# Substitution of 32-wide blocks: GpSimd in place of VectorE

## The chip, the cores and the metric

The kernel runs on one core of a Trainium2 chip. The metric is the device time of one execution in microseconds (us). A core has five engines that run their own queues of instructions, each in the order in which the program holds them: TensorE (PE in the profile; its weight loads are listed apart as PEld), VectorE (DVE), ScalarE (ACT), GpSimd (POOL) and SyncE (SP), which here only issues DMA transfers. Semaphores order the engines among each other.

## The reference

One transformer block on x of shape (8, 256, 256): 8 sequences of 256 tokens of 256 channels. A layernorm with shift and scale from a condition vector, a gated linear-attention layer, a gated residual, a second such layernorm, a feed-forward layer with 2:4 sparsified hidden values, and a second gated residual. What matters here is the recurrence of the attention layer, for 16 key heads, each with two value heads of width 128:

```python
def step(S, inp):
    q_t, k_t, v_t, b_t, d_t = inp
    Sk = jnp.einsum('bhi,bhipj->bhpj', k_t, S)
    dv = b_t[..., None] * (v_t - Sk)
    upd = jnp.einsum('bhi,bhpj->bhipj', k_t, dv)
    S = S * d_t[:, :, None, :, None] + upd
    o = jnp.einsum('bhi,bhipj->bhpj', q_t, S)
    return (S, o)
```

with q and k from a projection, a causal convolution of four taps and an l2 norm, v from projection and convolution, b a sigmoid, and d a decay between 0 and 1. The output o is rms-normed, multiplied by a gate silu(z) and projected back.

## The kernel before

The kernel does not step through the tokens. It cuts each sequence into chunks of 128 tokens and solves each chunk as a triangular system: with a strictly triangular matrix A of products of keys, decays and b, it needs the inverse of (I + A). That inverse is built in two parts. First, the 32 x 32 blocks on the diagonal of all matrices of a group are inverted by substitution; then two levels of small matmuls join blocks of 32 to blocks of 64 and blocks of 64 to 128.

The work is ordered in groups. A group is four key heads (GH = 4) of a pair of sequences; there are 4 pairs and 16 heads, so 16 groups. A head of a pair has 2 sequences x 2 chunks x 2 value heads = 8 matrices, a group 32, and each matrix has four diagonal blocks of 32: 128 blocks, one for each partition. The steps, by the names in the code:

- stage_a, for each head: the key projection (ps_k, L432), the convolution (convolved: one ScalarE instruction at L418 and three VectorE instructions at L420), the norms, the table diag (GpSimd, L516) and the power nk (GpSimd, L523), the scan e (VectorE, L551), and the matrices a_t (L563). The diagonal blocks of a_t are written to a scratch area scr in device memory (L572).
- stage_b, once for each group: one load (L585) brings the 128 blocks, each as a 32 x 32 square in its own partition, into the tile blk; GpSimd sets the diagonal (L587); then 30 steps of substitution follow, step j with two VectorE instructions: tmp, the outer product of j values of column j and 31 - j values of row j (L604), and its subtraction from the block of j rows and 31 - j columns (L610). Each instruction needs the result of the one before it. After step 16 and after the last, the helper turn lets ScalarE write a transposed negative copy xb (L592) and a negated blk (L597); after the last, SyncE issues the stores of both to scr_x (L596) and scr_y (L599).
- levels, for two heads at a time: loads of the inverted blocks from scr_x and scr_y (x_even at L690 and others), then matmuls ps_w (L707, L710), ps_t, ps_w2 and ps_t2, with the finished inverses in t_inv.
- prepare, for each head: projections of query and values (ps_qv, L432) with their convolutions cv (L418, L420), the gate (ps_z, L646; gz, L653), and a scale eps_q (GpSimd, L657).
- attend, for each head and sequence: matmuls with the inverse (L804, L847) and others, sums of squares ss (VectorE, L858), the reciprocal root rs (GpSimd, in the helper at L105), and the product of output, rs and gate og (VectorE, L871).
- shares and turned: the output projection (ps_y, L901), added to y (L912).
- feed_forward, for the tokens of sequences whose attention is complete: its work is spread over later groups; in it the VectorE instructions of the sparsification (L211 to L229). It uses the same GpSimd helper at L105 for rstd. The last pair's feed-forward runs alone at the end.

While the heads of one group are in attend, stage_a and stage_b of the next group are mixed in as background: the function along, called once for each round of the heads' generators, advances the background by a work count, in which a yield of stage_a counts 3.0 and a step of the substitution 1.0, so that it is due by the middle of the group. The levels for the first two heads of a group run within the last head of the group before, the levels for the other two in its second head. The order in which the instructions of an engine finally stand is fixed when the program is built, by a scheduler that goes by the order of the code and by its own timing of each instruction (L1210). The first group has nothing to be mixed with: its stage_a runs step by step in first_group, its substitution follows at once, and the heads' first projections are tied behind it with issue_after.

Of the kernel before, what the change touches and what calls it, by code (L numbers as in the profile page):

```python
# [48 lines left out]
def adaln_block(  # L49
# [18 lines left out]
    nc = tc.nc  # L68
# [297 lines left out]
    with ExitStack() as scope:  # L366
# [210 lines left out]
        def stage_b(scr, scr_x, scr_y):  # L577

            blk = single.tile([P, Q, Q], F32, tag="blk", name="blk")
            nc.sync.dma_start(out=blk, in_=scr)  # L585
            xb = single.tile([P, Q, Q], F32, tag="xb", name="xb")
            nc.gpsimd.memset(blk.rearrange("p a b -> p (a b)")[:, :: Q + 1], -1.0)  # L587
            yield

            def turn(rows):  # L590

                nc.scalar.activation(  # L592
                    xb[:, rows], blk[:, :, rows].rearrange("p b a -> p a b"), AF.Copy, scale=-1.0
                )
                if rows.stop == Q:
                    nc.sync.dma_start(out=scr_x, in_=xb)  # L596
                nc.scalar.activation(blk[:, :, rows], blk[:, :, rows], AF.Copy, scale=-1.0)  # L597
                if rows.stop == Q:
                    nc.sync.dma_start(out=scr_y, in_=blk)  # L599

            for j in range(1, Q - 1):
                m = Q - 1 - j
                tmp = single.tile([P, j, m], F32, tag="tmp", name="tmp", bufs=2)
                nc.vector.tensor_tensor(  # L604
                    out=tmp,
                    in0=blk[:, j, None, j + 1 :].to_broadcast([P, j, m]),
                    in1=blk[:, 0:j, j, None].to_broadcast([P, j, m]),
                    op=ALU.mult,
                )
                solved = nc.vector.tensor_tensor(  # L610
                    out=blk[:, 0:j, j + 1 :], in0=blk[:, 0:j, j + 1 :], in1=tmp, op=ALU.subtract
                )
                yield solved.ins
                if j == Q // 2:
                    turn(slice(0, Q // 2))
            turn(slice(Q // 2, Q))
            yield
# [321 lines left out]
        def first_group(filled, recs, scratch):  # L939
# [34 lines left out]
            for done in stage_b(scr, *scratch):  # L974
                last[0] = done or last[0]

        def ahead(g, recs, scratch):

            bp, k0 = groups[g]
            scr = scratch_of(scratch)  # L980
            h_bp = tokens(bp)
            wk = single.tile([P, GH, CC, P], F32, tag="wk", name="wk")
            nc.sync.dma_start(out=wk, in_=w_keys[k0 // GH])

            waiting = []
            for hp in range(GH + 1):
                if hp < GH:
                    waiting.append(stage_a(k0 + hp, bp, hp, wk, h_bp, scr))
                    recs.append(next(waiting[-1]))
                    yield 3.0  # L990
                if hp > 0:
                    for _ in waiting.pop(0):
                        yield 3.0
            for done in stage_b(scr, *scratch):
                last[0] = done or last[0]
                yield 1.0
# [217 lines left out]
```

## Time and profile before

| | |
|---|---|
| median of 3 runs | 2111.28 us (2106.41 to 2114.01) |
| the profiled execution's own time | 2106.59 us |
| its span, first to last instruction | 2104.6 us |
| mean granted TensorE clock | 0.991 of full speed |
| TensorE busy | 2000.5 us (95%) |
| VectorE busy | 1666.0 us (79%), 4039 instructions |
| ScalarE busy | 1271.3 us (60%) |
| GpSimd busy | 391.1 us (19%), 376 instructions |

A busy time is the time in which at least one instruction of that engine was on record; matmuls are pipelined, and their ends are modelled. A row of a group names line, engine, operation, output and inputs by the program's names, shapes and count, then the busy time in us and the mean duration of one in ns, and behind the second bar the idle time of the engine just before these instructions and what ended it. A row of stretches gives for each engine the busy time and, in brackets, the number of instructions. A row of a timeline gives the start in us, the duration in us, and in square brackets the idle time before and what ended it; a row may cover several instructions in succession.

### The profile page before, as it was taken

How to read it: one execution, taken by the hardware profiler on the slowest of the kernel's cores; microseconds unless marked ns; L12 is line 12 of the kernel's file. 1: busy time of each engine (PE TensorE's matmuls, PEld its weight loads, DVE VectorE, ACT ScalarE, POOL GpSimd, SP SyncE). 2: the span in 40 equal slices, each digit the busy share in tenths (PEclk: the TensorE clock that was granted, in tenths of full speed). 3: DMA queues.
4: the chain of work that ended last, by engine and by line, in shares of the span. 5: the costliest groups of instructions: out<-in, count | busy, mean ns of one | idle time of the engine just before them, and what ended most of it. 6: DMA issues, size and time to landing. Idle time of an engine off the chain costs nothing. (4 is left out here: it accounts for less than half of the span.)

```text
span 2104.6 us, 45727 instructions
## 1 busy us (share of the span) xinstructions
PE 2000.5 (95%) x16684; PEld 1583.3 (75%) x16684; DVE 1666.0 (79%) x4039; ACT 1271.3 (60%) x4260; POOL 391.1 (19%) x376
## 2 busy tenths in 40 slices
PE   8999999899999999999999989999999999999998
PEld 5567777677778777777777777777777877777877
DVE  6778887878788787788878779787978869787557
ACT  3557677766656556566665655657566655656652
POOL 3121312112121211212021121211213121121110
PEclk9999999999999999999999999999999999999999
DMA  4342414333343544434444443443444343344226
GB/s 127 99 131 72 117 55 108 99 80 105 92 115 103 125 115 102 123 105 111 140 92 111 107 123 113 114 115 99 128 110 115 97 127 110 94 121 116 66 91 218
DMA packets 356257, 230.99 MB, mean 110 GB/s; under 512 B 286265, under 2 KB 297913, under 8 KB 356033
## 3 DMA queue, kind: packets, MB, share of 16 engines
q1 hardware_dynamic: 336160, 167.53, 30.7%
q10 hardware_dynamic: 19872, 60.54, 9.3%
q8 instruction: 132, 2.16, 0.4%
q14 instruction: 93, 0.75, 0.1%
HBM read 188.38 MB, written 29.12 MB: 103 GB/s over the span
## 5 line engine op out<-in xcount | busy, mean ns | idle before, releaser
L420 DVE SCALAR_TENSOR_TENSOR cv<-ps_qv,conv_sb,cv 128x510 f32<-128x510 f32 (+2 forms) x564 | 409.4, 739 | 88.1 <-ACT cv L418 84.4
L432 PE MATMUL ps_qv<-h_bp,wh 128*128 128x512 f32 x768 | 365.7, 602 | 8.4 <-DVE cv L420 7.1
L105 POOL TENSOR_TENSOR rs<-ss,minus_halves 128x4 f32<-128x4 f32 x128 | 147.9, 1163 | 942.3 <-DVE ss L858 941.8
L646 PE MATMUL ps_z<-wh,h_bp 128*128 128x256 f32 x1024 | 252.1, 387 | 17.7 <-DVE cv L420 17.2
L901 PE MATMUL ps_y<-wo,og_p 128*128 128x256 f32 x1024 | 236.3, 380 | 2.6 <-ACT gz L653 2.2
L646 PEld LDWEIGHTS ps_z<-wh,h_bp 128*128 128x128 f32 x1024 | 186.9, 193 | 49.1 <-DVE cv L420 22.4
L838 ACT ACTIVATE junk<-o 128x128 f32<-128x128 f32 x512 | 154.2, 305 | 112.1 <-DVE o L854 96.8
L432 PEld LDWEIGHTS ps_qv<-h_bp,wh 128*128 128x128 f32 x768 | 134.3, 193 | 112.7 <-issue 100.2
L901 PEld LDWEIGHTS ps_y<-wo,og_p 128*128 128x128 f32 x1024 | 188.2, 190 | 27.7 <-ACT gz L653 3.3
L604 DVE TENSOR_TENSOR tmp<-blk 128x30 f32<-128x30 f32 (+14 forms) x480 | 156.9, 327 | 56.4 <-DMA blk<-scr 48.7
L418 ACT ACTIVATE cv<-ps_qv,conv_sb 128x512 f32<-128x512 f32 x188 | 129.3, 689 | 107.5 <-PE ps_qv L432 106.8
L516 POOL TENSOR_TENSOR diag<-consts,bk 128x1032 f32<-128x1032 f32 x64 | 123.5, 1929 | 364.5 <-DVE bk L507 329.1
L420 DVE SCALAR_TENSOR_TENSOR k_t<-ps_k,conv_sb,k_t 128x510 f32<-128x510 f32 (+1 forms) x189 | 139.8, 741 | 37.6 <-ACT k_t L418 35.6
L610 DVE TENSOR_TENSOR blk<-blk,tmp 128x30 f32<-128x30 f32 (+14 forms) x480 | 156.8, 327 | 9.6
L551 DVE TENSOR_TENSOR_SCAN e<-dbc,diag 128x1032 f32<-128x1032 f32 x60 | 138.1, 2302 | 19.5 <-POOL diag L516 13.4
L871 DVE SCALAR_TENSOR_TENSOR og<-o,rs,gz 128x128 f32<-128x128 f32 x512 | 145.8, 344 | 8.4 <-POOL rs L105 7.7
L812 PE MATMUL ps_ks<-u,cross 128*128 128x128 f32 x1024 | 141.7, 280 | 7.1 <-ACT u L806 3.9
L812 PEld LDWEIGHTS ps_ks<-u,cross 128*128 128x128 f32 x1024 | 128.7, 193 | 16.6 <-issue 6.3
L190 PE MATMUL ps_ff<-h,w_ff 128*128 128x128 f32 x1024 | 132.5, 277 | 4.2 <-ACT h L149 2.3
L190 PEld LDWEIGHTS ps_ff<-h,w_ff 128*128 128x128 f32 x1024 | 124.4, 192 | 14.9 <-issue 5.9
L778 ACT ACTIVATE vn<-ps_v,nk 128x256 f32<-128x256 f32 x256 | 104.5, 486 | 51.4 <-PE ps_v L773 51.2
L826 ACT ACTIVATE o<-ps_ks,g_in 128x128 f32<-128x128 f32 x256 | 79.9, 365 | 87.2 <-DVE rr L817 78.5
(180 smaller groups left out, 4189.9 us busy)
## 6 DMA issues: line engine op xcount, KB each, us to landing
wh<-in_w_heads ACTq DMA_DIRECT2D x64, 640.0 KB, 4.5
w_ff<-in_w_ff SPq DMA_DIRECT2D x128, 256.0 KB, 3.1
dbc<-d_dram SPq DMA_DIRECT2D x60, 516.0 KB, 3.7
wo<-in_w_heads ACTq DMA_DIRECT2D x32, 512.0 KB, 3.7
w_dn<-in_w_down SPq DMA_DIRECT2D x64, 256.0 KB, 3.0
wk<-in_w_keys SPq DMA_DIRECT2D x16, 512.0 KB, 3.5
scr<-a_t SPq DMA_DIRECT2D x256, 32.0 KB, 2.1
blk<-scr SPq DMA_DIRECT2D x16, 512.0 KB, 4.5
```

Of the source, the lines that this page charges most:

```text
L105: nc.gpsimd.tensor_tensor(out=out, in0=in_, in1=minus_halves[:, :n], op=ALU.pow)
L190: nc.tensor.matmul(ps[:, a, l, :], lhsT=w[:, k, l, :], rhs=h2[:, k, :], start=(k == 0), stop=(k == CC - 1),)
L420: nc.vector.scalar_tensor_tensor(out=dst[:, :, d:], in0=ps[:, :, : T - d], scalar=taps[:, KC - 1 - d : KC - d], in1=dst[:, :, d:], op0=ALU ...
L432: nc.tensor.matmul(ps.rearrange("p b t -> p (b t)"), lhsT=w[k], rhs=h_bp[:, k, :], start=(k == 0), stop=(k == CC - 1),)
L551: nc.vector.tensor_tensor_scan(e.rearrange("p i s t -> p (i s t)"), dbc.rearrange("p i f -> p (i f)"), diag.rearrange("p s t -> p (s t)"), ...
L604: nc.vector.tensor_tensor(out=tmp, in0=blk[:, j, None, j + 1 :].to_broadcast([P, j, m]), in1=blk[:, 0:j, j, None].to_broadcast([P, j, m]), ...
L610: solved = nc.vector.tensor_tensor(out=blk[:, 0:j, j + 1 :], in0=blk[:, 0:j, j + 1 :], in1=tmp, op=ALU.subtract)
L646: nc.tensor.matmul(ps[:, n, :], lhsT=h_bp[:, k, i * T + n * P : i * T + (n + 1) * P], rhs=wh[:, k * 640 + 384 : (k + 1) * 640], start=(k = ...
L812: nc.tensor.matmul(ps_ks[:, ct, h, :], lhsT=cross[:, h, ct, :], rhs=u0[:, h, :], start=True, stop=True)
L838: nc.scalar.activation(junk, o[:, n, h, :], AF.Square, accum_out=ss[:, n, h : h + 1])
L871: nc.vector.scalar_tensor_tensor(out=og[:, n, h, :], in0=o[:, n, h, :], scalar=rs[:, 2 * n + h : 2 * n + h + 1], in1=gz[:, i, n, h, :], op ...
L901: nc.tensor.matmul(ps_y[:, n, :], lhsT=og_p[:, j // 2, i, n, j % 2, :], rhs=wo[:, j // 2, j % 2, :], start=(j == 0), stop=(j == 3),)
```

## The change

The two instructions of a substitution step are issued to GpSimd (nc.gpsimd) where they were issued to VectorE (nc.vector). Operands, shapes and the order of the code stay as they are.

```diff
             for j in range(1, Q - 1):
                 m = Q - 1 - j
                 tmp = single.tile([P, j, m], F32, tag="tmp", name="tmp", bufs=2)
-                nc.vector.tensor_tensor(
+                nc.gpsimd.tensor_tensor(
                     out=tmp,
                     in0=blk[:, j, None, j + 1 :].to_broadcast([P, j, m]),
                     in1=blk[:, 0:j, j, None].to_broadcast([P, j, m]),
                     op=ALU.mult,
                 )
-                solved = nc.vector.tensor_tensor(
+                solved = nc.gpsimd.tensor_tensor(
                     out=blk[:, 0:j, j + 1 :], in0=blk[:, 0:j, j + 1 :], in1=tmp, op=ALU.subtract
                 )
                 yield solved.ins
```

## The prediction

> **What bounds the kernel now.** I read the page's busy times and groups first, then the busy times of single stretches, the waits, and the timeline at both ends of the substitution.
>
> ```profile
> PE 2000.5 (95%) x16684; PEld 1583.3 (75%) x16684; DVE 1666.0 (79%) x4039; ACT 1271.3 (60%) x4260; POOL 391.1 (19%) x376
> ...
> L604 DVE TENSOR_TENSOR tmp<-blk 128x30 f32<-128x30 f32 (+14 forms) x480 | 156.9, 327 | 56.4 <-DMA blk<-scr 48.7
> ...
> L516 POOL TENSOR_TENSOR diag<-consts,bk 128x1032 f32<-128x1032 f32 x64 | 123.5, 1929 | 364.5 <-DVE bk L507 329.1
> ...
> L610 DVE TENSOR_TENSOR blk<-blk,tmp 128x30 f32<-128x30 f32 (+14 forms) x480 | 156.8, 327 | 9.6
> ```
>
> TensorE carries the span, and no other engine is near it on average. POOL looks empty, and DVE would lose 156.9 + 156.8 = 313.7 us. But an average says nothing of the stretch in which the substitution runs. Its 960 instructions come in 16 bursts of 60 (one per group). The first burst stands alone in the startup; the 15 others I cut out by the first and last L604/L610 of each and asked for the busy times of those stretches, first all instructions (two stretches and the sum shown), then those on blk alone (the sum):
>
> ```profile
> core 0: us, PE busy (x) PEld busy (x) DVE busy (x) ACT busy (x) POOL busy (x), PEclk, DMA share, GB/s
> 147.10:191.60 44.50, 40.51 (x259) 32.53 (x259) 40.77 (x124) 31.69 (x104) 4.99 (x7) 1.00 0.12 32
> 1385.90:1427.30 41.40, 40.36 (x259) 32.74 (x259) 38.60 (x121) 24.65 (x86) 6.24 (x8) 1.00 0.38 110
> sum 640.80, PE 608.99 PEld 496.30 DVE 597.48 ACT 396.54 POOL 85.51; mean PE 40.60 PEld 33.09 DVE 39.83 ACT 26.44 POOL 5.70
> ...
> sum 640.80, DVE 293.39 ACT 26.25 POOL 2.28; mean DVE 19.56 ACT 1.75 POOL 0.15
> ```
>
> A stretch lasts 640.8/15 = 42.7 us on average. In it DVE is busy 39.8 us (93%), 19.6 of them with the substitution; POOL has 5.7. So in a third of the span DVE is as full as TensorE, and it is there that the change acts. TensorE is idle 640.8 - 609.0 = 31.8 us in all the stretches together: the most that a freer DVE can give back there.
>
> What hangs on the end of a burst is the next thing to see. At 1427 us (ScalarE's and SyncE's timelines):
>
> ```profile
> 1427.34 1.10 ACT L592 ACTIVATE xb<-blk 128x512 f32<-128x512 f32 x1 [1.36 <-DVE blk L610]
> ...
> 1428.47 0.32 SPq L596 DMA_DIRECT2D scr_x<-xb  x1
> 1429.61 0.32 SPq L599 DMA_DIRECT2D scr_y<-blk  x1
> 1431.11 1.83 SPq L690 DMA_DIRECT2D x_even<-scr_x  x4
> ```
>
> ScalarE sits waiting for the last L610, copies, the copy goes out, and the load of x_even follows as soon as it can; the levels' matmuls (L707, L710), which open the next group's work, wait for that load 14.2 us in total by the answer for L690 (6.1, 3.2, 2.8 and 2.1). The burst's end is thus on the path, with next to no slack: a burst that ends later moves the levels, and before them ScalarE (other copies are queued behind L592) and SyncE's queue (the loads behind L596).
>
> **What a substitution step costs on POOL.** The trace has two POOL multiplies of the same make (one input repeated along rows, the other along elements): diag, 1032 elements, median 1918 ns, and taps, 512 elements, 1041 ns (L1012). The line through them is 177 ns + 1.687 ns per element. One burst is two instructions of j(31 - j) elements for j = 1 to 30, that is 2 x 4960 = 9920 elements: 60 x 0.177 + 9920 x 0.001687 = 10.6 + 16.7 = 27.4 us, against 19.6 on DVE. Every step needs the one before; the trace shows no POOL instruction that waits for its predecessor on POOL. Bounds: 0 (nk follows diag without a gap) and 0.1 us (rs starts 0.09 us after the ss that DVE wrote); DVE's own chain has 0.03. I take 0.05: 3.0 us, so 30.4 us per burst, 0.51 per step. The upper bound for the fixed part is eps_q (L657), a POOL instruction of 4 elements with mean 387 ns (24.8 us for 64): 60 x 0.21 = 12.6 us more. The rows of a step are short (30 rows of one element at j = 30) and diag's are 129 long; no row prices that, and this upper end has to cover it.
>
> The Trainium skill, "GPSIMD Engine Reference", section 3, holds VectorE to be about 1.96 times faster for two-input elementwise work; by that ratio a burst would be an estimated 19.6 x 1.96 = 38 us instead of 30, and the final time some 120 us higher than mine. The diag row is of this very kernel, so I keep it.
>
> **What the move makes late.** On POOL a step shares the queue with rs, eps_q and rstd, and it shares something with DVE:
>
> ```profile
> 370.29 1.92 POOL L516 TENSOR_TENSOR diag<-consts,bk 128x1032 f32<-128x1032 f32 x1 [1.45 <-DVE bk L507]
> ...
> 370.66 1.58 DVE L500 TENSOR_SCALAR n2k<-n2k 128x4 f32<-128x4 f32 x1
> ...
> 1971.06 3.27 POOL L105 TENSOR_TENSOR rs<-ss,minus_halves 128x4 f32<-128x4 f32 x2 [20.41 <-DVE ss L858]
> ...
> 1971.70 0.42 DVE L223 TENSOR_TENSOR mag<-mag,c 128x256 f32<-128x256 f32 x1
> 1972.03 0.42 DVE L224 SCALAR_TENSOR_TENSOR mag<-mag,c 128x256 f32<-128x256 f32 x1
> ```
>
> The DVE instruction of 4 elements takes 1.58 us (others of its kind 0.16) and ends with diag; in the other direction two rs take 3.27 us (about 1.03 each elsewhere) while DVE works through a run of instructions whose inputs all lie in SBUF. DVE instructions with an input in PSUM (cv L420, 742 ns beside POOL and 740 without) show nothing of it. So POOL and DVE's all-SBUF instructions exclude each other. The same page, section 8, says that the two share their SBUF interfaces, with contention for DVE instructions of two SBUF inputs; that speaks against this change, which puts 60 such POOL instructions in each stretch that until now had about seven.
>
> How much: in the stretch 1385.9 to 1427.3, DVE's all-SBUF instructions besides the substitution are og 4.6 us, the sparsification and feed-forward tail (L168 to L253) 5.5, ss 0.6: 10.7 us. In the four stretches before the first feed-forward there are only og and ss, 5.2. Mean (11 x 10.7 + 4 x 5.2)/15 = 9.2 us in which POOL stands still.
>
> **The sum for a stretch.** POOL: 30.4 + 5.7 (its own work) + 9.2 (locked out) = 45.3 us against the 42.7 that the stretch lasts: 2.6 us longer, times 15 = 39 us. DVE falls from 39.8 to 20.3 us plus its waits for a POOL step in progress (some 12 runs of all-SBUF instructions at up to 0.45 us, 5 us): it has room, and the rs that are late by a step or more are caught by that room, except where og (L871) waits at the head of DVE's queue with cv behind it; POOL's length counts that already. Of TensorE's 31.8 us idle in the stretches I give back 10: the waits view puts only some of it on DVE (cv 17.2 + 7.1 in the whole span), the rest on ScalarE and loads.
>
> **The startup.** The first burst runs from 60.6 to 83.8 us, almost by itself (19.9 of 23.2 us), and its levels start at 89.9. On POOL it takes 30.4 + 1.6 (two rstd and an eps_q between) = 32 us: 9 us later. TensorE has key projections of the next group to bring forward (it does them at 86.3), but they are bounded by ScalarE's and DVE's part; I count all 9, bounds 3 and 22 (with the upper end of the step's cost). The final feed-forward holds no substitution: 0.
>
> Sum: 39 + 9 - 10 = +38 us on 2106.6, the profiled execution's own time (span 2104.6 and 2 us around it): 2144.6. The median of the three runs lies 4.7 us above that execution, so the forecast for the median is 2149 us.
>
> **Rivals.** *POOL keeps up* (faster). Place: the same 15 stretches. If a step averages under (42.7 - 5.7 - 9.2)/60 = 0.46 us, handoff included, POOL ends no later than DVE did, and nothing is left but the relief of DVE: TensorE's idle time in the stretches shrinks by 20 to 31.8 us, less 7 for the startup: 2111.3 - 13 to - 25, say 2092. For it: my step without a handoff is 0.457; DVE's 93% there. Against: 0.457 is the least that the rows give, and short rows and exclusion only add. *POOL is far slower than diag suggests* (the bound for the fixed part): 12.6 more per burst, 15 x 15.2 = 228 + 22 - 10: 2351. *It cancels*: relief of 10 against the startup's 9, with the stretches hidden under TensorE's other work (it does next-group matmuls at 1450 to 1457, while the levels run): 2111. That the change leaves work on DVE can be excluded: both instructions are named in the diff.
>
> **Numbers.** Forecast case, slower, 0.55 (its own range 2118 to 2290); far slower 0.08; cancels 0.10; faster 0.27. About 0.3% (6 us) is what a measurement can tell from no change. The range for 8 in 10 goes from 2088 (nearly all of TensorE's idle time in the stretches) to 2290 (70% of the way from the forecast to the far slower case).
>
> **What would show it.** Right: L604 and L610 on POOL at means of 440 to 480 ns, POOL near 19% + 440/2105 = 40%, DVE near 64%; bursts of 44 to 48 us; more waiting of ScalarE's L592 and of L707 for x_even; og waiting for rs well over 7.7 us; rs mean above 1163. Wrong: bursts shorter than 42 us and cv no longer ahead of TensorE's waits (the faster rival), or step means over 600 ns (the slow one). My forecast falls if TensorE's stalls do not follow the burst's end.

## The result, and the profile after

| | median of runs | ratio to before, 95% interval |
|---|---|---|
| before | 2112.65 us (2106.41 to 2114.69, 4 runs) | |
| after | 2136.98 us (2130.84 to 2147.15, 4 runs) | 1.0125 [1.0079, 1.0171] |

The change costs 24 us. The forecast was 2149 us. The profiled execution took 2134.93 us, with a span of 2132.5 us. The page of the kernel after, its busy times and groups:

```profile
PE 2007.0 (94%) x16684; PEld 1585.4 (74%) x16684; DVE 1471.3 (69%) x3079; ACT 1270.7 (60%) x4260; POOL 862.1 (40%) x1336
...
L105 POOL TENSOR_TENSOR rs<-ss,minus_halves 128x4 f32<-128x4 f32 x128 | 130.7, 1025 | 501.2 <-DVE ss L858 500.4
L610 POOL TENSOR_TENSOR blk<-blk,tmp 128x30 f32<-128x30 f32 (+14 forms) x480 | 254.9, 531 | 35.8
...
L604 POOL TENSOR_TENSOR tmp<-blk 128x30 f32<-128x30 f32 (+14 forms) x480 | 241.0, 502 | 34.8
...
L871 DVE SCALAR_TENSOR_TENSOR og<-o,rs,gz 128x128 f32<-128x128 f32 x512 | 178.2, 408 | 91.7 <-POOL rs L105 91.3
```

Each of the two instructions of a step takes 502 or 531 ns instead of 327, and POOL stands at 40%. DVE lost 314 us of steps but only 195 us of busy time: og, for one, went from 344 to 408 ns. TensorE's busy time rose by 6.5 us with the same matmuls, and its idle time (span less busy) from 104.1 to 125.5 us. The busy times of the 15 stretches of the substitution (the first two and the sum):

```profile
core 0: us, PE busy (x) PEld busy (x) DVE busy (x) ACT busy (x) POOL busy (x), PEclk, DMA share, GB/s
155.10:195.90 40.80, 37.42 (x238) 30.48 (x236) 26.08 (x61) 30.32 (x101) 34.75 (x67) 1.00 0.12 35
277.30:318.30 41.00, 35.66 (x221) 27.78 (x220) 26.01 (x54) 27.94 (x94) 34.58 (x67) 1.00 0.13 36
...
sum 603.10, PE 545.67 PEld 448.38 DVE 377.97 ACT 351.16 POOL 524.41; mean PE 36.38 PEld 29.89 DVE 25.20 ACT 23.41 POOL 34.96
```

A stretch is 603.1/15 = 40.2 us long, not longer than the 42.7 of before. Yet TensorE is idle in the stretches for 603.1 - 545.7 = 57.4 us, against 31.8. DVE, now busy 25.2 us of a stretch, is no longer full. The view of the waits of the kernel after (us in total, times, longest) shows who waits in its place:

```profile
POOL rs L105 <- DVE ss L858: 500.4, 58, 28.3
...
DVE og L871 <- POOL rs L105: 91.3, 46, 7.1
ACT xb L592 <- POOL blk L610: 72.7, 22, 7.4
```

Before, the same two waits of og and xb were 7.7 and 13.0 us. The two traces show one thing more. Laid over each other in order of time, at least 2766 of TensorE's 16684 matmuls stand elsewhere than before, 752 of ScalarE's 4260 instructions and 638 of the 3079 that VectorE has beside the steps. The scheduler that fixes the order goes by its own timing of each instruction, so that a slower step can redraw the program. My prediction had no term for that.

### The profile page after: what moved, and what is told of

Same layout as the page of the kernel before. It is cut to its first block, busy times and chain, and to the rows that moved or that the text cites. A ratio compares the mean times of both kernels' runs of the same rounds, so it can differ in the third digit from the quotient of the medians.

```text
span 2132.5 us, 45638 instructions
## 1 busy us (share of the span) xinstructions
PE 2007.0 (94%) x16684; PEld 1585.4 (74%) x16684; DVE 1471.3 (69%) x3079; ACT 1270.7 (60%) x4260; POOL 862.1 (40%) x1336
## 3 DMA queue, kind: packets, MB, share of 16 engines
q1 hardware_dynamic: 336160, 167.53, 30.9%
## 4 chain that ended last, share of the span: by engine, by line
PE 39%; DVE 22%; POOL 17%; DMA 9%; ACT 6%; issue 6%; SPq 2%; ACTq 0%; DVEq 0%; POOLq 0%
PE ps_qv L432 6%; POOL blk L610 6%; POOL tmp L604 6%; PE ps_z L646 5%; DVE cv L420 4%; PE ps_y L901 4%; DVE e L551 3%; PE ps_k L432 3%; PE ps_ks L812 3%; DMA blk<-scr 3%; DVE a_t L563 3%; DVE og L871 3%; POOL diag L516 2%; PE ps_ff L190 2%; DVE k_t L420 2%
## 5 line engine op out<-in xcount | busy, mean ns | idle before, releaser
L105 POOL TENSOR_TENSOR rs<-ss,minus_halves 128x4 f32<-128x4 f32 x128 | 130.7, 1025 | 501.2 <-DVE ss L858 500.4
L610 POOL TENSOR_TENSOR blk<-blk,tmp 128x30 f32<-128x30 f32 (+14 forms) x480 | 254.9, 531 | 35.8
L604 POOL TENSOR_TENSOR tmp<-blk 128x30 f32<-128x30 f32 (+14 forms) x480 | 241.0, 502 | 34.8
L901 PE MATMUL ps_y<-wo,og_p 128*128 128x256 f32 x1024 | 241.2, 386 | 2.7 <-ACT gz L653 2.5
L871 DVE SCALAR_TENSOR_TENSOR og<-o,rs,gz 128x128 f32<-128x128 f32 x512 | 178.2, 408 | 91.7 <-POOL rs L105 91.3
L778 ACT ACTIVATE vn<-ps_v,nk 128x256 f32<-128x256 f32 x256 | 103.4, 480 | 34.8 <-PE ps_v L773 34.6
```

The source lines that it names most:

```text
L604: nc.gpsimd.tensor_tensor(out=tmp, in0=blk[:, j, None, j + 1 :].to_broadcast([P, j, m]), in1=blk[:, 0:j, j, None].to_broadcast([P, j, m]), ...
L610: solved = nc.gpsimd.tensor_tensor(out=blk[:, 0:j, j + 1 :], in0=blk[:, 0:j, j + 1 :], in1=tmp, op=ALU.subtract)
L871: nc.vector.scalar_tensor_tensor(out=og[:, n, h, :], in0=o[:, n, h, :], scalar=rs[:, 2 * n + h : 2 * n + h + 1], in1=gz[:, i, n, h, :], op ...
L901: nc.tensor.matmul(ps_y[:, n, :], lhsT=og_p[:, j // 2, i, n, j % 2, :], rhs=wo[:, j // 2, j % 2, :], start=(j == 0), stop=(j == 3),)
```

## The experiments

The column us gives the difference of the medians. Each kernel is compared with runs of the kernel before on the same chip.

| kernel | steps on | queues in the order | us | ratio, 95% interval |
|---|---|---|---|---|
| after | POOL | its own | +24 | 1.0125 [1.0079, 1.0171] |
| e1_first_only | POOL in burst 1, else DVE | its own | +27 | 1.0125 [1.0111, 1.0139] |
| e2_not_first | DVE in burst 1, else POOL | its own | +30 | 1.0140 [1.0121, 1.0159] |
| e3_none | none | its own | +6 | 1.0030 [1.0017, 1.0042] |
| e4_unread_pool | POOL, end unread | its own | +25 | 1.0109 [1.0092, 1.0126] |
| e6_root_dve | POOL, roots on DVE | its own | +27 | 1.0125 [1.0105, 1.0145] |
| e7_root_dve_before | DVE, roots on DVE | its own | +21 | 1.0098 [1.0081, 1.0115] |
| e9_code_order | POOL, tied to the roots | its own | +30 | 1.0148 [1.0127, 1.0169] |
| e11_second_third | POOL in bursts 2 and 3 | its own | +2 | 1.0014 [0.9997, 1.0030] |
| e12_order_of_before | POOL | that of before | +28 | 1.0137 [1.0120, 1.0154] |
| e13_order_of_after | DVE | that of after | +49 | 1.0243 [1.0221, 1.0266] |
| e15_none_order_of_before | none | that of before | -49 | 0.9776 [0.9760, 0.9793] |
| e16_roots_ahead | POOL, roots earlier | that of before | +29 | 1.0138 [1.0121, 1.0155] |

### Parts of the change, each with a newly drawn order

Two kernels split the change between the startup and the rest (e2 has False for True), one drops the steps, one keeps them but lets nobody wait for the burst's end. The code cuts are shortened:

```diff
-                nc.gpsimd.tensor_tensor(
+                eng.tensor_tensor(            # eng = nc.gpsimd if (bursts[0] == 0) == True else nc.vector
```

> Only the first burst (startup) goes to GpSimd, the other 15 stay on VectorE. Startup theory: its end comes 11 us later and its levels 13 us later in the trace of the changed kernel, with little behind which that could hide, so 9 to 13 us slower than before (ratio 1.004 to 1.006). Theories that put the loss into the other 15 bursts (roots behind steps in POOL's order; ScalarE waiting for the end of a burst; exclusion): 0 to 4 us slower.

> All bursts but the first go to GpSimd. Startup theory: 11 to 15 us slower than before (what is left of 24). Theories of the other 15 bursts: 20 to 25 us slower.

```diff
-                nc.gpsimd.tensor_tensor(out=tmp, ...)
-                solved = nc.gpsimd.tensor_tensor(...)
-                yield solved.ins
+                yield set_diag.ins
```

> Leaves out the 30 steps of every substitution; loads, diagonal, copies and stores stay. Gives the floor under both kernels. If VectorE's load in the stretches costs TensorE something, 2060 to 2075 us (23 us of startup and 15 to 30 of idle time in the stretches); if only the startup's burst counts, 2085 to 2092 us. Either way the distance from here to the changed kernel is what the steps cost on GpSimd.

```diff
-                    xb[:, rows], blk[:, :, rows].rearrange("p b a -> p a b"), AF.Copy, scale=-1.0
+                    xb[:, rows], consts[:, None, :Q].to_broadcast([P, Q // 2, Q]), AF.Copy, scale=-1.0
...
-                nc.scalar.activation(blk[:, :, rows], blk[:, :, rows], AF.Copy, scale=-1.0)
+                nc.scalar.activation(xb[:, :, rows], consts[:, None, : Q // 2].to_broadcast([P, Q, Q // 2]), ...)
...
-                    nc.sync.dma_start(out=scr_y, in_=blk)
+                    nc.sync.dma_start(out=scr_y, in_=xb)
```

> The changed kernel, but ScalarE's two copies read a constant table in place of blk, so that nobody waits for the end of a burst; the steps run on GpSimd as before. Burst-end theory (ScalarE's queue and the levels wait for the last step): within 5 us of the kernel without steps. Theory of the roots behind steps, and of exclusion: 25 to 35 us above the kernel without steps.

None came out as a theory of one place would have it. The startup alone costs 27 us and the other 15 bursts alone 30, and together they cost 24. Without any step, and thus without 314 us of DVE's work, the kernel is 6 us slower than before. With nobody waiting for the end of a burst (e4) the loss stays: it is 18 us above e3, where the burst-end theory had at most 5 and the others 25 or more. So the burst's end, on which my sum rested, is not what makes e4 slow; for after that is not shown, since e4 has an order of its own (at least 4069 of its matmuls stand elsewhere than in after).

Next came the roots: rs and rstd, which stand in POOL's queue between the steps. A VectorE multiply of the same size was put in their place (no root is computed), once with the steps on POOL, once with the steps on VectorE, and in a third kernel each step was tied behind the root that stands before it in the code:

```diff
-        nc.gpsimd.tensor_tensor(out=out, in0=in_, in1=minus_halves[:, :n], op=ALU.pow)
+        nc.vector.tensor_tensor(out=out, in0=in_, in1=halves[:, :n], op=ALU.mult)
```

> The changed kernel, with the reciprocal root (rs, rstd) left out: one VectorE multiply of the same size stands in its place, so that POOL's queue holds no roots that og or xn wait for. Root theory (rs stands behind substitution steps in POOL's fixed order and holds VectorE at og): og's waiting for rs, 91 us, is gone, and the time comes within 6 us of the next kernel. Exclusion theory (VectorE's all-SBUF instructions and POOL's steps shut each other out): 15 to 20 us above the next kernel. Burst-end theory: the same.

> The kernel before, with the same replacement of the root by a VectorE multiply: the reference point for the run above. All theories: within 8 us of before, since og waits there for rs only 7.7 us.

```diff
+                with tc.issue_after(roots[-1]):
                     nc.gpsimd.tensor_tensor(out=tmp, ...)
                     solved = nc.gpsimd.tensor_tensor(...)
```

> The changed kernel, with every substitution step tied behind the last root that precedes it in the code, so that fewer steps can be put ahead of a root in POOL's order. Root theory: og waits for rs clearly less than 91 us, and the kernel is 5 to 15 us faster than the changed one. Exclusion theory: no difference over 5 us. Burst-end theory: slower, since bursts end later.

e7 is the warning: no step moves, the roots leave the idle engine, and the kernel loses 21 us, in a newly drawn order (2533 matmuls elsewhere than before). Beside it e6 is 6.6 us slower, near what the root theory had, but two orders are compared there as well (3485 matmuls apart), so it decides nothing. e9 left TensorE's and ScalarE's queues as in after, but og still waited 85.7 us for rs (91.3 in after): the tie did not free the roots, and the time stayed as it was. One more kernel comes out nearly in the order of before:

```diff
+            eng = nc.gpsimd if bursts[0] in (1, 2) else nc.vector
```

> GpSimd takes only the second and third burst, the rest stays on VectorE. In the trace with all bursts but the first on GpSimd, the attention of these two groups ran 7 and 6 us ahead of before, and everything later fell behind. If these two groups are where an empty VectorE helps (no feed-forward beside them), 3 to 7 us faster than before; if any new order of the program costs what the startup run showed, 5 us or more slower.

Here 458 of TensorE's matmuls stand elsewhere than before, and the time is the same (twelve runs). So a newly drawn order had to be kept apart from the engine.

### The order held

The program is built twice. The first build, with the steps on the one engine, records in which order the instructions stand in the queues of TensorE, VectorE, ScalarE and SyncE; the second, with the steps on the other engine or without them, ties each instruction behind its predecessor of the first. These ties are orders within one queue and add no semaphore.

```diff
+        for engine, names in follow.items():
+            last = None
+            for name in names:
+                i = now[name]
+                if last is not None:
+                    tc.add_manual_dep(i, last.name, DependencyInfo(NoSync, DATA), reason="order")
+                last = i
...
+    _, order = built("vector", None)
+    nc, _ = built("gpsimd", order)      # e13: "gpsimd", then "vector"; e15: "vector", then no steps
```

> The changed kernel with the queues of TensorE, ScalarE, SyncE and (substitution steps aside) VectorE held to exactly the order that they have in the kernel before; the steps stand on GpSimd. Order theory (what costs is the other order that the scheduler writes once any timing changes, as the root and first-burst runs suggest): 0 to 10 us slower than before, most of it the startup's. Engine theory (GpSimd's longer chain, the roots behind steps, exclusion): 20 us slower or more.

> The kernel before (steps on VectorE) with the queues of TensorE, ScalarE, SyncE and (steps aside) VectorE held to exactly the order that they have in the changed kernel. Order theory: 15 to 25 us slower than before, like the changed kernel. Engine theory: within 6 us of before.

> Leaves out the 30 steps of every substitution, with the four queues held to the order that they have in the kernel before. What VectorE's 313 us of steps really cost there: if their load matters in the stretches, 15 to 40 us faster than before; if they are hidden, 0 to 15 us faster, the startup's burst included.

Both simple theories fall. In the order of before the steps cost 28 us more on POOL than on DVE; in the order of after they cost 25 us *less* (24 against 49). e3 and e15 issue the same instructions and stand 54 us apart. The order that the scheduler drew for POOL's timing is bad for DVE's steps (49). The reverse is not shown: POOL's steps stand at +28 in the order of before and at +24 in their own, and the intervals overlap. The order of before is even better for the kernel without steps (e15) than the one drawn for it (e3). The page of e13 and its waits show what the order of after does to DVE's steps:

```profile
PE 2017.1 (94%) x16684; PEld 1594.2 (74%) x16684; DVE 1661.8 (77%) x4039; ACT 1268.9 (59%) x4260; POOL 375.3 (17%) x376
```

```profile
ACT xb L596 <- DVE blk L614: 48.4, 12, 6.7
...
PEld ps_w L711 <- DMA x_even<-scr_x: 18.4, 10, 4.5
...
PE ps_w L711 <- DMA x_even<-scr_x: 13.7, 9, 3.7
```

In e13 ScalarE waits for the burst's end (xb), and the levels' first matmul (L711 there) waits 18.4 + 13.7 = 32.1 us for x_even behind it, as my sum had it for after. In after itself the same line (L707) waits for x_even for 6.5 + 2.2 = 8.7 us, against 6.1 + 3.2 = 9.3 before (after, then before):

```profile
PEld ps_w L707 <- DMA x_even<-scr_x: 6.5, 9, 1.2
...
PE ps_w L707 <- DMA x_even<-scr_x: 2.2, 5, 0.8
```

```profile
PEld ps_w L707 <- DMA x_even<-scr_x: 6.1, 7, 2.2
...
PE ps_w L707 <- DMA x_even<-scr_x: 3.2, 3, 2.0
```

So what was to be the cost of a later burst's end did not grow.

### Where the 28 us go in the order of before

In e12 the matmuls stand in the order of before (10 of 16684 records apart), so the two traces can be read side by side, matmul by matmul. This is one such place in the middle of a burst. DVE's timeline of the kernel before (start, us, instruction, idle time before it):

```profile
1399.32 0.16 DVE L858 SCALAR_TENSOR_TENSOR ss<-ss,eps_q 128x4 f32<-128x4 f32 x1 [0.35 <-ACT junk L838]
...
1400.71 1.14 DVE L871 SCALAR_TENSOR_TENSOR og<-o,rs,gz 128x128 f32<-128x128 f32 x4
...
1402.74 0.41 DVE L854 TENSOR_TENSOR o<-o,ps_o 128x256 f32<-128x256 f32 x1
```

The same instructions on DVE in e12 (its lines are numbered 4 higher):

```profile
1416.26 0.16 DVE L862 SCALAR_TENSOR_TENSOR ss<-ss,eps_q 128x4 f32<-128x4 f32 x1 [0.82 <-ACT junk L842]
1422.05 2.87 DVE L875 SCALAR_TENSOR_TENSOR og<-o,rs,gz 128x128 f32<-128x128 f32 x4 [5.62 <-POOL rs L109]
...
1425.51 0.41 DVE L858 TENSOR_TENSOR o<-o,ps_o 128x256 f32<-128x256 f32 x1
```

From ss to the start of og it is 1.4 us before and 5.8 in e12, and og's four take 2.87 us instead of 1.14. POOL's timeline of e12 shows why:

```profile
1416.29 0.59 POOL L614 TENSOR_TENSOR blk<-blk,tmp 128x210 f32<-128x210 f32 x1
...
1420.40 0.64 POOL L614 TENSOR_TENSOR blk<-blk,tmp 128x234 f32<-128x234 f32 x1
1421.00 1.02 POOL L109 TENSOR_TENSOR rs<-ss,minus_halves 128x4 f32<-128x4 f32 x1
1421.98 0.61 POOL L608 TENSOR_TENSOR tmp<-blk 128x238 f32<-128x238 f32 x1
```

The root's input is ready at 1416.42, but the root stands behind a row of steps, each waiting for the last, and starts at 1421.00. DVE meanwhile stands with og at its head. Behind og are the cv and the o that empty PSUM for TensorE, and TensorE's timeline of e12 has the end of that chain:

```profile
1421.37 1.89 PE L248 MATMUL ps_out<-w_dn,hid 128*128 128x256 f32 x8
1425.97 0.93 PE L789 MATMUL ps_kq<-cv,k_t 128*128 128x256 f32 x2 [2.70 <-DVE o L858]
```

The same matmul of before starts at 1403.00, right behind the ps_out ahead of it, and waits for nothing. And the 2.70 us are not all. Busy times of e12 by 3.4 us (the last three columns are TensorE's clock, DMA share and GB/s):

```profile
core 0: us, PE busy (x) PEld busy (x) DVE busy (x) ACT busy (x) POOL busy (x), PEclk, DMA share, GB/s
...
1422.90:1426.30 3.40, 0.70 (x4) 0.31 (x3) 3.40 (x7) 2.96 (x7) 3.01 (x6) 1.00 0.56 154
1426.30:1429.70 3.40, 3.40 (x15) 3.13 (x14) 3.02 (x7) 3.40 (x18) 3.14 (x5) 0.50 0.01 2
1429.70:1433.10 3.40, 3.40 (x22) 3.09 (x22) 3.40 (x9) 2.35 (x6) 3.08 (x5) 1.00 0.14 18
```

After a slot in which TensorE was busy for 0.70 of 3.40 us, its clock is halved for the next slot, which holds 15 matmuls; the one after it, at full clock again, holds 22. I laid the clock's record over the matmuls of before, after and e12 (without the first 30 us): of 40 slots of 3.41 us at full clock with TensorE busy less than half the time, 34 were followed by a slot at half clock; of 1750 others at full clock, 2. In 9 of these 36 places the half clock lasted a second slot. All of these slots with 2 us or more of idle time are among the 34. So a stall of 2 us or more in one slot is paid again with up to 1.7 us for each slot at half clock. The Trainium skill, "TensorE: Matmul & The Clock Gate", Part 1, has a free-running window of 3413 ns and a clock that is either whole or half, and the trace agrees; its rule of thumb, no idle gaps over about 3.4 us, is too mild here, where one gap of 2.70 us was enough.

The account of the kernels (span, TensorE busy, the rest idle; the last column is one minus the granted clock, times the span, and an upper limit of what the clock can have cost):

| | granted clock | span | busy | idle | clock |
|---|---|---|---|---|---|
| before | 0.991 | 2104.6 | 2000.5 | 104.1 | 18.9 |
| e11 | 0.991 | 2102.7 | 1999.3 | 103.4 | 18.9 |
| after | 0.988 | 2132.5 | 2007.0 | 125.5 | 25.6 |
| e12 | 0.983 | 2135.5 | 2009.8 | 125.7 | 36.3 |
| e16 | 0.986 | 2130.0 | 2004.9 | 125.1 | 29.8 |
| e13 | 0.982 | 2151.7 | 2017.1 | 134.6 | 38.7 |
| e3 | 0.988 | 2110.7 | 2017.6 | 93.1 | 25.3 |
| e15 | 0.995 | 2055.2 | 1979.0 | 76.2 | 10.3 |

The 30.9 us of e12's span are 21.6 us more idle time and 9.3 us more busy time. Of the idle time 9.5 us arise in the startup, up to the first group's first ps_u (at 109.9 us before, at 123.2 in e12), and 11.9 later (the rest is rounding). Among the waits that grew later are these, in the waits of TensorE (e12, then before; before has none of ps_z for junk):

```profile
PE ps_kq L789 <- DVE o L858: 15.4, 5, 5.0
...
PE ps_z L650 <- ACT junk L455: 6.8, 2, 3.9
...
PE ps_u L808 <- DVE aq L798: 5.8, 5, 2.5
```

```profile
PE ps_kq L785 <- DVE o L854: 2.4, 2, 1.5
...
PE ps_u L804 <- DVE aq L794: 1.8, 4, 0.8
```

The chain shown above is the first of them: five stalls, 15.4 us in all, against 2.4 before. Ahead of each of the five stands an og that has waited 4.3 to 5.7 us for rs.

### The roots put ahead

If that chain is the cause, roots that don't stand behind steps should give its part back. e16 is e12 with POOL's own queue rewritten too: 46 of the 158 roots go in front of the steps that started after the root's input was ready.

```diff
+    pool = once["EngineType.Pool"]
+    for k, j in AHEAD:
+        pool.insert(j, pool.pop(k))
+    nc, _ = built("gpsimd", {**order, "EngineType.Pool": pool})
```

> The kernel with steps on GpSimd and the other four queues in the order of before, with one difference in POOL's own queue: each of the 46 roots (of 158) that stood behind steps which began after its input was ready is put ahead of those steps, 154 places in all. The first run of that kernel lost 13 us in the startup's burst and about 17 over the other 15. Root theory: og's waiting for rs falls from 88 us to 30 or less, and 8 to 17 us of the 28 to before come back (about 2120 to 2128 us). Exclusion and burst-end theories: og waits less, but the time stays within 5 us of 2136.

It comes out as e12. TensorE's waits in e16 have lost the chain, and others have come up:

```profile
PE ps_z L652 <- DVE cv L426: 19.4, 18, 3.0
...
PE ps_z L652 <- ACT junk L457: 7.0, 2, 4.0
...
PE ps_kq L791 <- ACT vn L784: 5.7, 3, 2.0
...
PE ps_kq L791 <- DVE o L860: 1.4, 1, 1.4
```

The wait of ps_kq for o went from 15.4 to 1.4 us, og's wait for rs only from 87.9 to 59.5, not to the 30 that was expected. ScalarE's wait for the burst's end (xb) rose from 55.8 to 70.2: a root that is put ahead pushes the steps behind it back. TensorE's extra idle time after the startup falls only from 11.9 to 10.5 us. The time stayed within 5 us of 2136, as the rival theories had it. So the chain from the root to ps_kq is seen in the trace, but its price is not shown: nearly all of it went, and the time did not fall by more than the interval of some 3.5 us. A likely reading, not tested by itself, is that POOL has both the roots and the steps on the path, and that putting one ahead delays the other. Left beside it are a step that is slow by itself and DVE's instructions stretched beside it; these were not taken apart.

## Why the prediction was right or wrong

- **Direction and size** held: +24 us against a forecast of +38, inside the range. The way there was only in part the one that I described; that the sum came out near is in part luck.
- **Cost of a step**: somewhat low. Predicted 0.457 us for an instruction and a handoff of 0.05; measured 0.517 us (the sign was 440 to 480 ns, the rows have 502 and 531) and 0.08 (in the startup, L604 runs for 0.61 us from 76.53 and its L610 starts at 77.22). Per burst 31.1 + 4.8 = 35.9 us instead of 30.4. POOL's 40%, the later startup (the first levels 13 us later, predicted 9), more waiting of og and of xb came as written; DVE came to 69%, not 64. The ratio of one instruction to DVE's is 517/327 = 1.58, against 27.4/19.6 = 1.40 by my rows and the 1.96 of the Trainium skill, "GPSIMD Engine Reference", section 3, that I had weighed against them.
- **The step that failed: "2.6 us longer, times 15 = 39 us".** A stretch measured 40.2 us. Its parts: steps and handoffs 35.9 (I had 30.4), POOL's own work 3.9 (5.7), and locked out at most 2, already within these (9.2). I had the lock the wrong way round. Measured against the median of like instructions, POOL's were stretched by some 30 us in the whole run, no more than before (14 us of it are steps), and DVE's by some 80 us against 18 before: DVE pays for the sharing. Nor do POOL and DVE simply exclude each other, as I read the lines: og takes 344 ns beside rs as well as alone, before and after, and some 600 to 640 beside a step. The signs I named for it (rs mean over 1163, measured 1025; bursts of 44 to 48 us; L707 waiting more for x_even) all failed; the bursts are even shorter than the 42 us that I had as a sign of the faster rival.
- **"Except where og waits at the head of DVE's queue ... POOL's length counts that already."** I costed this half sentence at nothing beyond POOL's length. Read in the same order (e12), a delay does go from a root behind steps to og, to o, to a PSUM bank, to ps_kq: a stall in the middle of a burst, whatever the burst's length, 13 us more than before in all. That it makes the kernel slower is not shown, since e16 without most of it is no faster. In after the levels' wait for the burst's end did not grow, and I had said that the forecast falls if TensorE's stalls do not follow that end. What the +24 us of after consist of in its own order stays open; shown is what the move costs with the order held, 28 us, and that 9.5 us of e12's idle time lie in the startup.
- **Not in the sum: the clock.** I priced a stall at its length. In these traces a slot with a stall of over 2 us is followed by a slot at half clock. Of the +28 us span of after up to 6.7 go there, of e12's +31 up to 17.4.
- **Not in the sum: the order.** Most edits of the timing made the scheduler draw another program (e9 and e11 hardly did). The order alone moves this kernel by tens of us (e13 against before: 49; e3 against e15: 54). After is +24 in its own order and +28 in that of before; that these are so near is no proof that the order did nothing, since the same steps on DVE differ by 49 between the two.
- **The relief of DVE, "10" of at most 31.8**: the limit counted idle time alone. With the steps gone and the order kept (e15) the kernel gains 49 us: 28 of idle time of TensorE in the whole span, and 21 of its busy time, for which I had no term (up to 8.6 of them are the clock). These 49 us hold both, the load on DVE and the waiting for the steps; the two were not parted. On POOL the steps' cost in that order rises from 49 to 77 us.

How the delay builds up, by the start of each group's first ps_u (L804) against before, in us: e12 has +13.3 in the first group, +16.9 in the fifth, +18.9 in the ninth, +25.0 in the thirteenth, +30.8 at the end: the startup is never caught up, and each later burst adds some 1.1 us. After has +17.4, +5.0, +17.6, +22.2 and +27.8: its own order makes the startup good within two groups and loses it again. Left open: why e1, whose steps are all on DVE after the startup, loses 11 us more in its second to fifth groups, and why the order of before, not chosen for it by anything that I found, suits DVE's steps so well. No kernel that does all the work beat the one before; e11 is equal to it.

## What to carry to other kernels

An engine with little to do may still be the wrong place for a chain of dependent steps: look at what else stands in its queue and who waits at the head of another queue for that; the mean share of busy time and the length of the burst do not show it. Price a stall of the TensorE with the clock that it costs, not with its length alone. Where a scheduler draws the order of the program, measure a move twice, once freely and once with the queues held to the old order: otherwise the edit and the new draw are read as one.

## What the runs showed of the hardware

- Beside a stall, the clock: half for one or two slots of 3.41 us after a slot in which TensorE was busy less than half the time (34 of 40 such slots at full clock, 2 of 1750 others).
- A POOL instruction that needs the one before it on POOL starts some 0.08 us after its end, on DVE 0.03.
- Small products on POOL: 0.258 us for 30 elements a partition, 0.651 for 240 (means in after), thus 1.87 ns per element on a fixed part of 0.2 us; the subtraction in place 0.260 and 0.682, thus 2.0 ns.
- POOL's steps slow DVE's instructions whose operands all lie in SBUF: in after og takes 600 ns on average beside tmp and 639 beside blk, 344 alone. POOL's small rs does not (343). Where DVE reads a single tile it is held as well (n2k beside diag 1.58 us, alone 0.16, in before). In all DVE was stretched by some 80 us in after and 18 before. Instructions with an input in PSUM are not slowed (cv: mean 739 ns in both pages).
